# A decoder layer in one kernel: loads on other queues, norms beside the preceding cross-attention, another order of the first rows and another memory layout

## The chip, the cores and the metric

The kernel runs on one core of a Trainium2 chip. The metric is the device time of one execution in microseconds (us). Six actors matter. TensorE (PE) multiplies matrices; its weight loads (PEld) overlap its matmuls. VectorE (DVE) and ScalarE (ACT) do elementwise work and read PE's results out of PSUM. GpSimd (POOL) does some copies and, above all, issues DMAs; SyncE (SP) only issues DMAs. Each of them works through its own instructions in order, so that an instruction which waits holds up all that stand behind it on that engine. The 16 DMA engines of the core move the data.

## The reference: what is computed

`x` is 4 batches of 512 rows of 512 numbers. Three blocks with residuals are added to it:

```python
x = x + attn(layernorm(x), Wq, bq, Wk, bk, Wv, bv, Wo, bo)   # 16 heads of 128
x = x + gamma * xattn(layernorm(x), ctx, ctx)                # 8 heads over 64 rows each
x = x + ffn(layernorm(x), w1, w3, w2)                        # hidden 1365
```

- The self-attention takes, for each head, the softmax over a 128 x 128 matrix: `q` and `k` are contracted over the 512 positions, not over the head's numbers.
- The cross-attention treats each batch as a 512 x 512 matrix, cut into 8 heads of 64 rows. A head's scores are 512 x 512, contracted over its 64 rows.
- In the feed-forward block (FFN) each weight matrix is first made ternary: with s the mean absolute value, `q = clip(round(w / s), -1, 1) * s`. Then `silu(x w1) * (x w3)`, times w2.

## The kernel before, in words

**Number format.** Products that need it are made from three parts of each operand (`h`, `l`, `d`, class `Tri`): one pass of `h` and `l` matmuls into one PSUM bank, one of `d` into another, joined by `total` (L357) on DVE. `products` (L330) does this for a 512 x 512 product in two pairs of row blocks; it is 48 matmuls. At six points in it, it calls `tick()`, through which other work is woven in.

**First phase (`phase_a`).** For each batch `b` the rows are normalized (`normed`, L375) and stored to DRAM (`kept_x`); then a Gram matrix is formed (`gram_upper`, L407, and `gram_rest`, L435). Batch 0 is normalized chunk by chunk under a fixed order on DVE, the other batches at once. Then follow 16 steps (`STEPS`, L858, head group `j` outside, batch `b` inside). A step forms `keys_of` (L470) from the Gram matrix and the key weights, then, one step later, the `scores` (L490) with the query weights and a softmax, and one more step later the transposed result is stored to DRAM (`kept_e`). Weights are loaded by `raw_of` (L232): a 512-row matrix in four chunks of 128 rows by four runs of 512 bytes, and a row `last` that is broadcast. The last chunk's row 127 is then overwritten with the bias by a small DMA from POOL. `fold` (L252) adds a multiple of `last` to each chunk on DVE. Query chunks of the next head group are loaded by SP when the step with `b == 0` has issued its scores, and folded (`queries_folded`, L851) in the step with `b == 1`, after `keys_of`. The value and output weights are cut into their parts beside the steps (`kept_weights`, L276) and stored to DRAM.

**Second phase.** The loop from L966 goes over batches `b` and head groups `j`. Each turn has two products, `values_out` (L455, with the `o` weights) and `values_of` (L480, with the `v` weights); each reads 12 weight tiles of 256 KB, which SP loads into the pool `a_w`. Between them stands `output(*waiting)` (L536), which adds the preceding turn's result to four accumulator tiles `acc`; these start as `x` plus the bias `bo` (`accumulators`, L944, `biased`, L952). After the last head group, `acc` goes to DRAM (`x_a`).

Beside these products run, through `tick()`, two chains of small steps, paced by the class `Side` (L168): `n` steps over `of` ticks.

- `quantize()` (L639) reads the FFN weights twice in pieces through the pool `a_stage` (loads by POOL, `staged`, L571), makes them ternary and stores them.
- `row_norms` (L651) and `cross` (L670) of the *preceding* batch. `row_norms` takes the mean and deviation of each row from `acc`, stores them to DRAM (`norm_a`) and loads them back in another layout (`norms`), all on POOL's queue. `cross` then fetches rows `xd` and `kd` (`fetch`, L685), scales them (`split`, L692: ACT makes `qs` and `kh`, DVE corrects `qs` and makes `kl`), and for each of 8 heads makes scores `xs` (`softmax_rows`, L709), transposes the softmax and weighs the values. The 11 steps of norms and 62 of `cross` together are spread over the 48 ticks of a batch; `side.rest()` at `j == 0` finishes what is left.

**Third phase.** The FFN (L1043) multiplies each batch by `t1` and `t3` (L1058) and `t2` (L1093). The cross-attention of the last batch runs beside batches 0 and 1.

**Order of the work.** The program's order gives each instruction a priority; a scheduler at compile time then orders each engine's instructions by when it thinks their inputs are ready. `tc.issue_after(mark)` keeps what is in its block, as far as it is on the mark's own engine, behind the marked instruction. Pools lie on the left or right end of SBUF like stacks; a pool with `reuse_waits="tile"` that lies on another's former place waits only for the tiles it covers.

Of the kernel before, what the change touches and what calls it, by code (L numbers as in the profile page):

```python
# [11 lines left out]
F32 = mybir.dt.float32  # L12
# [22 lines left out]
H_OF = 1.0 - 0.5**13  # L35
PAD_RIGHT, WIDER = 88, 128


@with_exitstack
def decoder_layer_kernel(  # L40
# [111 lines left out]

    x3p, tp, ep = apool("a_x3", 12), apool("a_t", 3), apool("a_e", 3)
    kept = {
# [77 lines left out]
    def raw_of(n, j, pool, load, bufs):  # L232

        def bring(k):
            t = pool.tile([P, GW], F32, tag=f"raw_{n}", bufs=bufs, name=f"{n}_raw_{j}_{k}")
            load(heads(t), of_heads(w_of[n][:, ts(k, P), :], j))
            if k == KC - 1:
                bias = bqkv[:, ts(KINDS.index(n), GW)].rearrange("(o g) c -> g o c", o=1)
                nc.gpsimd.dma_start(heads(t[P - 1 :, :]), of_heads(bias, j))
            return t  # L240

        last = pool.tile([P, GW], F32, tag=f"last_{n}", bufs=1, name=f"{n}_last_{j}")
        load(heads(last), of_heads(w_of[n][:, D - 1 : D, :], j).to_broadcast([P, NG, DH]))
        return last, bring
# [31 lines left out]
    def kept_weights(pool):  # L276

        def load(dst, src):
            nc.gpsimd.dma_start(dst, src)

        def items():
            for j in range(HG):
                for k in range(KC):
                    yield "o", j, k, None
                for k in CHUNKS:
                    yield "v", j, k, None

        sources = {}

        def bring(n, j, k):  # L290
            if n == "o":
                t = pool.tile([P, GW], F32, tag="raw_v", bufs=3, name=f"o_raw_{j}_{k}")
                load(t, by_group(wo[j * T : (j + 1) * T, :], k))
                return t
            if k == KC - 1:
                sources[j] = raw_of("v", j, pool, load, 3)
            return sources[j][1](k)

        coming = []
        for item in itertools.chain(items(), [None]):  # L300
            if item is not None:
                coming.append((item[:3], bring(*item[:3])))
                if len(coming) < 2:
                    continue
            (n, j, k), t = coming.pop(0)
            gate = gates[0]
            if n == "v":
                fold(k, t, sources[j][0], gate)
            tri = Tri(
                *(pool.tile([P, GW], F32R, tag="made", bufs=5, name=f"{n}{p}_{j}_{k}") for p in "hld")  # L310
            )
            halves_of_weight(tri.h, tri.l, t, gate)
            third_of_weight(tri)
            for p, part in zip("hld", (tri.h, tri.l, tri.d)):
                nc.gpsimd.dma_start(kept[n, j, p][ts(k, P), :], part.bitcast(F32))
            yield
# [40 lines left out]
    def total(dst, h, d):  # L357

        nc.vector.scalar_tensor_tensor(dst, h, 1.0 + 1.0 / S, d, ALU.mult, ALU.add)  # L359

# [14 lines left out]
    def normed(b, xs, by_chunk):  # L375
# [3 lines left out]
        def finish(part, std):  # L379
            rstd = inverse(std, f"a_{b}_{part[0]}")  # L380
            for g in part:
                normalize(xs[g], xs[g], mv[:, g, 0:1], rstd[:, g - part[0] : g - part[0] + 1])
                nc.vector.memset(xs[g][:, D - 1 : D], 1.0)
                nc.gpsimd.dma_start(kept_x[b][ts(g, P), :], xs[g])
# [262 lines left out]
    CROSS_STEPS = 3 * 4 * NC + 14  # L647
    NORM_STEPS = 2 * NG + 3
    norms = {}

# [169 lines left out]
    def rows_given(b):  # L820
        return rows_of(b, xnp, "xn", [by_group(x[b], g) for g in range(NG)])

    xs = rows_given(0)

    mark["std"] = nc.scalar.activation(gam, eps, AF.Sqrt).ins
    idle_ones()
    with tc.manual_schedule(engines={nc.vector.engine}):
        normed(0, xs, True)
    make_identity(nc, ident)
# [5 lines left out]
    keys, queries, ys, es, grams, g3 = {j: {} for j in range(HG)}, {}, {}, {}, {}, {}  # L835
    grams[0] = gram_upper(0, xs)
    raw_k = raw_all("k", 0, krp)
    xs = rows_given(1)
    for k in range(KC):
        keys_halves(0, k, raw_k, gates[0])  # L840
    normed(1, xs, False)
    raw_q = raw_all("q", 0, qp)

    def first_rest():
        g3[0] = gram_rest(0, grams[0])

    grams[1] = gram_upper(1, xs, first_rest)
    keys_thirds(0)
    load(gam, gamma.to_broadcast([P, 1]))

# [13 lines left out]
    def turn(n):  # L864
        j, b = STEPS[n]
        turned(b, j, es.pop(n))

    for n, (j, b) in enumerate(STEPS):
        if n == 4:
            xpool.close()  # L870
            ovp = apool("a_ov", 1, phase_a, side="right")
            side = Side(kept_weights(ovp), KEPT_STEPS, 6 * (len(STEPS) - n) - 4)
        if n < 2:
            xs = rows_given(n + 2)
            normed(n + 2, xs, False)
        ys[n] = keys_of(b, j, g3[b], keys[j], side.tick)
        gates[0] = gate_of(ys[n][3])
        if n < 3:
            g3[n + 1] = gram_rest(n + 1, grams[n + 1])
        if n < 2:  # L880
            grams[n + 2] = gram_upper(n + 2, xs)
        if b == 1:
            queries_folded(j)
        if n > 0:
# [23 lines left out]
    def prepare_ffn(b, rows):  # L908
# [19 lines left out]


    u3p, mp = apool("a_u3", 12), apool("a_m", 4)  # L930
    accp, xnp, bop = apool("a_acc", 8), apool("a_xn_kept", 4), apool("a_bo", 1)
    cpool = [
# [5 lines left out]
        wpools.enter_context(tc.tile_pool(name=n, bufs=k, side="right", reuse_waits="tile"))  # L938
        for n, k in (("a_w", 21), ("a_stage", 3))
    )  # L940
    bo_bc = bop.tile([P, D], F32, name="bo_bc")
    nc.gpsimd.dma_start(bo_bc, bo.to_broadcast([P, D]))

    def accumulators(b):  # L944
        accs = []
        for g in range(NG):
            acc = accp.tile([P, D], F32, tag="acc", name=f"acc_{b}_{g}")
            nc.gpsimd.dma_start(acc, by_group(x[b], g))
            accs.append(acc)
        return accs  # L950

    def biased(accs):  # L952
        with tc.issue_after(mark["copied"]):
            for acc in accs:
                nc.vector.tensor_tensor(acc, acc, bo_bc, ALU.add)

    PRODUCT = 6
    TICKS = 2 * HG * PRODUCT
    quant = Side(quantize(), QUANTIZE_STEPS, B * TICKS - PRODUCT)
    side, waiting, accs = Side(), None, None  # L960

    def tick():
        quant.tick()
        side.tick()

    for b in range(B):  # L966
        for j in range(HG):
            u3 = values_out(b, j, x3, weights("o", b, j, wp), tick)
            if b == 0 and j == 0:
                turn(len(STEPS) - 2)  # L970
                turn(len(STEPS) - 1)
            if waiting:
                output(*waiting)
            if j == 0:
                side.rest()
                if b > 0:
                    side = Side(
                        itertools.chain(row_norms(b - 1, accs), cross(b - 1, *cpool)),
                        NORM_STEPS + CROSS_STEPS,
                        TICKS if b + 1 < B else TICKS - PRODUCT,  # L980
                    )
                accs = accumulators(b)
            if j == HG - 2:
# [3 lines left out]
            elif j == HG - 1:  # L987
# [3 lines left out]
                for _ in range(NC):  # L991
                    next(ffn_0)
            eT = turned_kept(b, j)
            ms = values_of(b, j, weights("v", b, j, wp), u3, tick)
            if j == 0:
                biased(accs)
            waiting = [b, j, eT, ms, accs]
    side.rest()
    quant.rest()
# [15 lines left out]
    def fpool(name, bufs):  # L1015
        return ctx.enter_context(tc.tile_pool(name=name, bufs=bufs, reuse_waits="tile"))

    f1, f3, f2, fwk, fg = (
        fpool("f_w1", 1), fpool("f_w3", 1), fpool("f_w2", 1), fpool("f_work", 2),
        fpool("f_g", 2 * NHC),  # L1020
    )
# [14 lines left out]
    for i in range(NHC):  # L1036
        r = min(P, HID - i * P)
        load(t2[:r, i, :].bitcast(F32), kept_t["w2"][i * P : i * P + r, :])
    side = Side(
        itertools.chain([None] * 9, cross(B - 1, *cpool)), CROSS_STEPS + 9, 2 * (NHC + NC) + 2  # L1040
    )

    for b in range(B):  # L1043
# [3 lines left out]
        for i in range(NHC):  # L1047
            if b + 1 < B and i == 2:
                if b + 2 == B:
                    side.rest()  # L1050
                coming = Side(prepare_ffn(b + 1, rows_f(b + 1)), PREPARE_STEPS, NHC - 3)
            r = min(P, HID - i * P)
            hs = []
            for t, n in ((t1, "h1"), (t3, "h3")):
# [10 lines left out]
                hs.append(ph)  # L1065
            sl = fwk.tile([P, T], F32, tag="sl", name=f"sl_{b}_{i}")
            mark["copied"] = nc.scalar.activation(  # L1067
                sl[:r, :], hs[0][:r, :], AF.Silu, scale=scales["w1"][:r, 2:3]
            ).ins
            gf = fwk.tile([P, T], F32, tag="gf", name=f"gf_{b}_{i}")  # L1070
            nc.vector.scalar_tensor_tensor(  # L1071
# [5 lines left out]
            g.append((gh, gl))  # L1077
            side.tick()
            coming.tick()
# [3 lines left out]
        for c in range(NC):  # L1083
            if b == B - 1:
                y = last_ys[c]
            else:
                y = fwk.tile([P, D], F32, tag="y", bufs=1, name=f"yo_{b}_{c}")
                load(y, x_c[b][ts(c, P), :])
# [12 lines left out]
            nc.sync.dma_start(out[b, ts(c, P), :], y)  # L1101
            side.tick()
            coming.tick()
# [47 lines left out]
```

## Time and profile before

| | us |
|---|---|
| Median of 3 runs (range) | 1228.7 (1222.69 to 1229.71) |
| The profiled execution's own time | 1230.62 |
| Its span | 1228.9 |

Busy time of the engines by stage (us), with PE's granted clock and what the DMAs moved:

| Stretch (us) | what runs | PE | DVE | ACT | clock | DMA GB/s |
|---|---|---|---|---|---|---|
| 0 to 33 | first rows | 25.80 | 26.96 | 11.53 | 0.95 | 298 |
| 33 to 120 | steps of head group 0 and on | 87.00 | 54.17 | 35.62 | 1.00 | 102 |
| 120 to 310 | the other head groups, `v` and `o` weights | 182.49 | 130.30 | 77.22 | 0.98 | 253 |
| 310 to 445 | second phase, batch 0 | 127.91 | 94.71 | 38.14 | 0.95 | 321 |
| 445 to 600 | batch 1, cross-attention of 0 | 137.32 | 121.39 | 85.46 | 0.93 | 251 |
| 600 to 770 | batch 2, cross-attention of 1 | 154.63 | 130.72 | 89.24 | 0.95 | 263 |
| 770 to 922 | batch 3, cross-attention of 2 | 138.40 | 113.05 | 86.44 | 0.98 | 222 |
| 922 to 1229 | FFN, cross-attention of 3 | 297.08 | 151.18 | 145.29 | 0.99 | 80 |

A line of the waits reads: engine, line and tile that waited, who ended the wait, then total, times and longest. A line of the timeline reads: start, duration, engine, line and operation, tile written and read, and in brackets the idle time of the engine before it and what ended it. "q" behind an engine's name marks its queue of issued work.

### The profile page before, as it was taken

The page shows a single profiled execution, that of the slowest core. Times are in us where ns is not written, and L with a number is a line of the kernel's source. Part 1 is how long each engine was busy: PE and PEld are TensorE (multiplying, and loading weights), DVE is VectorE, ACT ScalarE, POOL GpSimd, SP SyncE. Part 2 cuts the span into 40 slices and gives each one's busy share as a digit, 9 for nine tenths or more (in the row PEclk, how much of TensorE's full clock was granted, in tenths as well). Part 3 has the DMA queues.
Part 4 walks back from the last instruction along what each step waited for, and adds up shares of the span by engine and source line. Part 5 has one row for each costly group of instructions (what it writes and reads, how often), then busy time and mean ns, then how long its engine had stood idle before and what let it go on. Part 6 is the DMA issues. An engine that isn't in the chain of part 4 may idle for free. (4 is left out here: it accounts for less than half of the span.)

```text
span 1228.9 us, 16751 instructions
## 1 busy us (share of the span) xinstructions
PE 1150.6 (94%) x5406; PEld 888.6 (72%) x5406; DVE 822.5 (67%) x1766; ACT 568.9 (46%) x1141; POOL 312.4 (25%) x556
## 2 busy tenths in 40 slices
PE   7999999999899877999969999898998999999998
PEld 5788787878677655777737766665766877877886
DVE  8557776883667757878667897588875855625232
ACT  3344444532322225675336665275653769833120
POOL 2103444442211233221333322323202211100000
PEclk9999999999899987999979999989998999999999
DMA  9324878777998985878887878867747231121200
GB/s 292 111 60 153 278 239 263 237 255 261 365 316 296 349 306 160 274 233 267 279 270 234 277 236 285 281 212 233 225 161 243 86 112 44 44 94 43 86 9 35
DMA packets 126865, 252.07 MB, mean 205 GB/s; under 512 B 17140, under 2 KB 37924, under 8 KB 126778
## 3 DMA queue, kind: packets, MB, share of 16 engines
q1 hardware_dynamic: 91146, 140.54, 34.5%
q0 software_dynamic: 35632, 110.46, 27.3%
q8 instruction: 43, 0.70, 0.2%
q14 instruction: 44, 0.36, 0.1%
HBM read 196.40 MB, written 54.54 MB: 204 GB/s over the span
## 5 line engine op out<-in xcount | busy, mean ns | idle before, releaser
L1058 PE MATMUL h<-fxh,t 128*128 128x512 f32 (+1 forms) x352 | 141.4, 402 | 5.2 <-DMA t<-t_w 5.2
L1058 PE MATMUL h<-fxl,t 128*128 128x512 f32 (+1 forms) x352 | 139.0, 395 | 0.0
L727 ACT ACTIVATE p<-xs,xnmax 128x512 f32<-128x512 f32 x128 | 87.1, 687 | 62.2 <-PE xp L126 38.2
L721 DVE TENSOR_REDUCE xnmax<-xs 128x1 f32<-128x512 f32 x128 | 84.0, 685 | 15.4 <-PE xs L717 15.3
L1058 PEld LDWEIGHTS h<-fxh,t 128*128 128x128 f32 (+1 forms) x352 | 66.1, 188 | 21.6 <-issue 6.6
L716 PE MATMUL xs<-kh,qs 128*128 128x512 f32 x128 | 51.7, 405 | 30.8 <-DVE qs L700 30.4
L1058 PEld LDWEIGHTS h<-fxl,t 128*128 128x128 f32 (+1 forms) x352 | 66.0, 188 | 15.0 <-DVE acc L540 0.2
L539 PE MATMUL po<-m,eT 128*128 128x512 f32 x128 | 64.6, 649 | 9.0 <-DVE u L359 9.0
L496 PE MATMUL sc<-y,q_raw 128*128 128x128 f32 x512 | 63.0, 280 | 7.5 <-issue 5.1
L126 PEld LDWEIGHTS xp<-ident,p 128*128 128x128 f32 x512 | 59.1, 140 | 15.0 <-DVE acc L540 2.6
L496 PEld LDWEIGHTS sc<-y,q_raw 128*128 128x128 f32 x512 | 62.2, 196 | 10.7 <-issue 5.9
L1093 PE MATMUL y<-t,gh 128*128 128x512 f32 (+1 forms) x176 | 69.3, 394 | 0.0
L191 ACT ACTIVATE uh<-u 128x512 fp32r<-128x512 f32 x64 | 40.3, 631 | 62.5 <-DVE u L359 62.2
L126 PE MATMUL xp<-ident,p 128*128 128x128 f32 x512 | 67.6, 273 | 1.4 <-DVE acc L540 1.4
L1093 PE MATMUL y<-t,gl 128*128 128x512 f32 (+1 forms) x176 | 68.9, 391 | 0.0
L1071 DVE SCALAR_TENSOR_TENSOR gf<-h,scales_w,sl 128x512 f32<-128x512 f32 (+1 forms) x44 | 32.9, 748 | 52.4 <-PE h L1058 47.8
L129 ACT COPY pt<-xp 128x512 f32<-128x512 f32 x96 | 54.3, 591 | 26.8 <-PE xp L126 26.7
L1067 ACT ACTIVATE sl<-h,scales_w 128x512 f32<-128x512 f32 (+1 forms) x44 | 30.3, 689 | 72.6 <-PE h L1058 72.5
L760 PE MATMUL xo<-pt,vals 128*64 128x512 f32 x256 | 58.5, 599 | 0.0
L539 PEld LDWEIGHTS po<-m,eT 128*128 128x128 f32 x128 | 25.7, 207 | 41.1 <-issue 23.4
L679 POOL DMA_DIRECT2D xd<-x_a x64 | 33.9, 534 | 73.0 <-DVE qs L700 52.9
L717 PE MATMUL xs<-kl,qs 128*128 128x512 f32 x128 | 51.2, 402 | 1.2 <-DVE kl L704 1.1
(256 smaller groups left out, 3002.0 us busy)
## 6 DMA issues: line engine op xcount, KB each, us to landing
oh<-kept_oh SPq DMA_DIRECT2D x64, 256.0 KB, 6.4
ol<-kept_ol SPq DMA_DIRECT2D x64, 256.0 KB, 6.4
od<-kept_od SPq DMA_DIRECT2D x64, 256.0 KB, 5.0
vh<-kept_vh SPq DMA_DIRECT2D x64, 256.0 KB, 6.2
vl<-kept_vl SPq DMA_DIRECT2D x64, 256.0 KB, 6.1
vd<-kept_vd SPq DMA_DIRECT2D x64, 256.0 KB, 5.1
kd<-in_kv_dram POOLq DMA_DIRECT2D x64, 128.0 KB, 3.9
xd<-x_a POOLq DMA_DIRECT2D x64, 128.0 KB, 3.2
```

Of the source, the lines that this page charges most:

```text
L126: nc.tensor.transpose(pt[:, ts(k, P)], src[:, ts(k, P)], ident)
L129: nc.scalar.copy(dst, pv)
L191: nc.scalar.mul(tri.h, src, H_OF)
L496: nc.tensor.matmul(sc[:, ts(g, DH)], lhsT=w[k][:, ts(g, DH)], rhs=ys[k][:, ts(g, DH)], start=(k == 0), stop=(k == KC - 1),)
L539: nc.tensor.matmul(po, lhsT=eT[:, ts(g, DH)], rhs=ms[g], start=True, stop=True)
L716: nc.tensor.matmul(sc, lhsT=q[:, ts(m, P)], rhs=kh, start=True, stop=False)
L717: nc.tensor.matmul(sc, lhsT=q[:, ts(m, P)], rhs=kl, start=False, stop=True)
L721: nc.vector.reduce_max(nmax[:, i : i + 1], scs[i], axis=AX.X)
L727: nc.scalar.activation(p, scs[i], AF.Exp, bias=nmax[:, i : i + 1], scale=xscale, accum_out=den[:, i : i + 1],)
L760: nc.tensor.matmul(po[half, :], lhsT=vals[c][:, l, half], rhs=pt[j][:, l, :], start=(l == 0), stop=(l == NC - 1),)
L1058: nc.tensor.matmul(ph[:r, :], lhsT=t[:, block(i, k)], rhs=fxT[j][:, k, :], start=(k == 0 and j == 0), stop=(k == KC - 1 and j == 1),)
L1093: nc.tensor.matmul(py, lhsT=g[i][j][:r, ts(c, P)], rhs=t2[:r, i, :], start=(i == 0 and j == 0), stop=(i == NHC - 1 and j == 1),)
```

## The change

- `HOLE`: an unused tile of 18 KB a partition and `bo_bc` lie where `t3` of the FFN will lie; the pools `a_t` and `a_e` move to the right side, stay open, and serve the FFN's `sl`, `gf` and `y`, whose own pool goes away. `a_e` has 2 buffers in place of 3, `made` 6 in place of 5, `a_w` 18 in place of 21, `a_stage` 6 in place of 3.
- The last chunk of each `q`, `k` and `v` group is loaded without row 127 (127 rows).
- Batches 1 to 3 are normalized on ACT, with `-mean * rstd` as bias, and not on DVE.
- Rows of batches 1 and 2 are loaded ahead of the key weights, those of batch 3 ahead of the query weights; Gram matrices of batches 1 and 2 come ahead of the keys, that of batch 3 in step 1.
- In the steps with `b == 1` the queries are folded at the fourth tick of `keys_of`.
- `acc` and `bo_bc` are loaded by SP, a batch ahead; `biased` stands behind the last `total` on DVE and not behind an instruction of ACT. `kept_e` is loaded ahead of `values_out`.
- A third chain, `aside`, makes the norms and the first six steps of `cross` in 12 ticks, while `side` still runs the preceding batch's cross-attention; `side` then takes the remaining 56 steps over 48 ticks, from `j == 1` to `j == 0` of the next batch. What is left of batch 2's runs in the first nine ticks of the FFN. `quant` starts after the first `values_out`.

```diff
-    x3p, tp, ep = apool("a_x3", 12), apool("a_t", 3), apool("a_e", 3)
+    tp, ep = (
+        ctx.enter_context(tc.tile_pool(name=n, bufs=k, side="right", reuse_waits="tile"))
+        for n, k in (("a_t", 3), ("a_e", 2))
+    )
+    x3p = apool("a_x3", 12)
...
-            load(heads(t), of_heads(w_of[n][:, ts(k, P), :], j))
+            rows = P if k < KC - 1 else P - 1
+            load(heads(t)[:rows], of_heads(w_of[n][:, k * P : k * P + rows, :], j))
...
+            if not by_chunk:
+                mean = mv[:, :, 0:1].rearrange("p g s -> p (g s)")
+                nc.vector.scalar_tensor_tensor(mean, mean, -1.0, rstd, ALU.mult, ALU.mult)
             for g in part:
-                normalize(xs[g], xs[g], mv[:, g, 0:1], rstd[:, g - part[0] : g - part[0] + 1])
+                if by_chunk:
+                    normalize(xs[g], xs[g], mv[:, g, 0:1], rstd[:, g - part[0] : g - part[0] + 1])
+                else:
+                    nc.scalar.activation(
+                        xs[g], xs[g], AF.Identity, bias=mv[:, g, 0:1], scale=rstd[:, g : g + 1]
+                    )
...
+    xs += [rows_given(1), rows_given(2)]
     raw_k = raw_all("k", 0, krp)
-    xs = rows_given(1)
-    for k in range(KC):
-        keys_halves(0, k, raw_k, gates[0])
-    normed(1, xs, False)
+    xs += [rows_given(3)]
     raw_q = raw_all("q", 0, qp)
+    load(gam, gamma.to_broadcast([P, 1]))
+    normed(1, xs[1], False)
...
-    grams[1] = gram_upper(1, xs, first_rest)
+    grams[1] = gram_upper(1, xs[1], first_rest)
+    normed(2, xs[2], False)
+    for k in CHUNKS:
+        keys_halves(0, k, raw_k, gates[0])
     keys_thirds(0)
-    load(gam, gamma.to_broadcast([P, 1]))
+    grams[2] = gram_upper(2, xs[2])
...
-        ys[n] = keys_of(b, j, g3[b], keys[j], side.tick)
+        if n == 1:
+            normed(3, xs[3], False)
+        ys[n] = keys_of(b, j, g3[b], keys[j], ticks_with(4 if b == 1 else 0))
...
-        if b == 1:
-            queries_folded(j)
...
-        for n, k in (("a_w", 21), ("a_stage", 3))
+        for n, k in (("a_w", 18), ("a_stage", 6))
...
-            nc.gpsimd.dma_start(acc, by_group(x[b], g))
+            load(acc, by_group(x[b], g))
...
-        with tc.issue_after(mark["copied"]):
+        with tc.issue_after(mark["total"]):
...
-            u3 = values_out(b, j, x3, weights("o", b, j, wp), tick)
+            if b == 0 and j == 0:
+                wo_tiles = weights("o", b, j, wp)
+                accs = accumulators(0)
+                load(bo_bc, bo.to_broadcast([P, D]))
+            else:
+                if j == HG - 1 and b + 1 < B:
+                    next_accs = accumulators(b + 1)
+                eT = turned_kept(b, j)
+                wo_tiles = weights("o", b, j, wp)
+            u3 = values_out(b, j, x3, wo_tiles, tick)
...
-            if j == 0:
+            if j == 0 and b > 0:
+                aside.rest()
+                crossing = itertools.chain(row_norms(b - 1, accs), cross(b - 1, *cpool))
+                aside = Side(itertools.islice(crossing, AHEAD), AHEAD, 2 * PRODUCT)
+                accs = next_accs
+            if j == 1 and b > 0:
                 side.rest()
-                if b > 0:
-                    side = Side(
-                        itertools.chain(row_norms(b - 1, accs), cross(b - 1, *cpool)),
-                        NORM_STEPS + CROSS_STEPS,
-                        TICKS if b + 1 < B else TICKS - PRODUCT,
-                    )
-                accs = accumulators(b)
+                side = Side(crossing, NORM_STEPS + CROSS_STEPS - AHEAD, TICKS)
...
+    LEFT = (NORM_STEPS + CROSS_STEPS - AHEAD) * 3 * PRODUCT // TICKS
+    crossing = itertools.chain([None] * 11, cross(B - 1, *cpool))
+    before = Side(itertools.chain(side.steps, [None] * LEFT), LEFT, 9)
+    aside = Side(itertools.islice(crossing, AHEAD), AHEAD, 9)
...
+    last = Side(crossing, CROSS_STEPS - 6, 2 * (NHC + NC) + 2 - 9)
```

## The prediction

> **What bounds the kernel now.** I read the page first, then who TensorE (PE) waits for, then the timeline around its longest wait, then the busy times by stage. Busy shares and clock come first:
>
> ```profile
> span 1228.9 us, 16751 instructions
> PE 1150.6 (94%) x5406; PEld 888.6 (72%) x5406; DVE 822.5 (67%) x1766; ACT 568.9 (46%) x1141; POOL 312.4 (25%) x556
> PEclk9999999999899987999979999989998999999999
> ```
>
> PE is the bound: it idles 78.3 us of 1228.9. The change adds and removes no matmul, so it can only win idle time and the low clock that follows a long idle. Who ended PE's waits (total, times, longest, all in us but the times):
>
> ```profile
> PE xs L716 <- DVE qs L700: 30.4, 3, 17.1
> PE po L539 <- DVE u L359: 9.0, 2, 5.8
> PE pg L414 <- DVE xn L383: 5.5, 2, 5.1
> PE h L1058 <- DMA t<-t_w: 5.2, 1, 5.2
> PE sc L496 <- issue: 5.1, 2, 2.7
> ...
> PE sc L496 <- ACT oh L257: 2.4, 1, 2.4
> ```
>
> Three waits, one at the start of each batch's cross-attention, are 30.4 us of it. The timeline of the longest (start, duration, idle time before in brackets):
>
> ```profile
> 443.85 0.69 DVE L955 TENSOR_TENSOR acc<-acc,bo_bc 128x512 f32<-128x512 f32 x1 [5.67 <-DMA acc<-in_x_dram]
> ...
> 453.65 0.55 POOL L663 DMA_DIRECT2D norm_a<-mv_c  x1
> ...
> 460.07 1.40 POOL L666 DMA_DIRECT2D norms<-norm_a  x2 [4.60 <-DMA norm_a<-mv_c]
> ...
> 469.62 0.79 PE L716 MATMUL xs<-kh,qs 128*128 128x512 f32 x1 [17.14 <-DVE qs L700]
> ```
>
> Row norms go to DRAM and back: 453.65 to 469.62 is 16.0 us. Ahead of it DVE stood 5.67 us behind a bias add whose acc load was late. What the idle costs afterwards (PE busy; later PEclk, DMA share, GB/s), with one early stretch for the DMA price below:
>
> ```profile
> 10.00:20.00 10.00, 6.11 (x23) 3.75 (x21) 9.74 (x24) 4.65 (x10) 1.69 (x4) 1.00 1.03 342
> ...
> 460.00:470.00 10.00, 0.38 (x1) 0.38 (x2) 4.46 (x9) 2.87 (x5) 3.72 (x7) 0.50 0.63 204
> 470.00:480.00 10.00, 10.00 (x26) 5.85 (x26) 9.47 (x19) 5.32 (x9) 3.47 (x7) 0.72 0.28 79
> ```
>
> After the gap PE is busy 10 us at clock 0.72: 2.8 us more lost. Last, the query weights of one head group in the first phase:
>
> ```profile
> 121.65 2.52 SPq L199 DMA_DIRECT2D q_raw<-in_wq_dram  x4
> ...
> 127.10 0.52 POOL L239 DMA_DIRECT2D q_raw<-in_bqkv_dram  x1 [2.76 <-DMA q_raw<-in_wq_dram]
> ...
> 135.20 2.74 DVE L254 SCALAR_TENSOR_TENSOR q_raw<-q_last,gate,q_raw 128x512 f32<-128x512 f32 x4
> ```
>
> They are issued 13.5 us before their folds; sc then waits 2.4 to 2.7 us, three times.
>
> **The change, part by part.** The sum starts at the profiled execution: 1230.6 us with a span of 1228.9, which is 1.9 above the median of the runs, 1228.7.
>
> *1. Norms and start of the cross-attention.* The 17 first steps (11 of norms, 6 of fetch, settle and split) still run in the 12 ticks after the batch's first output; the first xs moves from tick 12 to tick 13, behind output(b,0). That alone is little: 8 matmuls at 0.23 and four fp32 ones in 1.9 (row at 793.67), some 3.7 us. The rest comes from the queues. The bias adds now stand behind total on DVE (before, the mark was an ACT instruction and ordered nothing there), which takes 5.67 and 2.5 us of waiting out of the chain; the 16 acc loads leave POOL (16 x 0.54 us issue); six stage buffers in place of three relieve POOL's waits for them (77.4 + 42.1 us), behind which norm_a, norms and xd queue, and DVE's (7.91 us at 628.86 in batch 2's gap). From batch 2 on, the preceding cross-attention runs on through these ticks and fills PE. In batch 1: norms' inputs ready near 440, plus 16.0, is 456; PE reaches xs at 452.5 + 3.7. The three waits are 30.4, and the low clock after them 2.8 (470 to 480), 3.3 (630 to 640: 7.02 busy at 0.53) and 2.8 (800 to 810: 8.60 at 0.67): 39.3. Ends: nothing to 39.3. I take 34, as batch 1 has no slack left.
>
> A rule here: acc loads took a median of 7.0 us on POOL, xn loads of the same size 4.3 on SP. The Trainium skill (DMA: Bandwidth & Descriptors, "Issuing engines are not separate DMA queues") says that all issuers share the same 16 DMA engines, so that moving a load saves only issue time. By it the 1 MB of accs per batch now stands ahead of 12 weight loads on SP, and part 1 would hold only through its order, not through bandwidth.
>
> *2. Late xd and pieces.* po's 9.0 are ACT waiting for xd (7.3 us at 799.12), DVE behind it; pu_2h's wait of 2.3 is DVE behind a weight piece (3.99 at 664.76). POOL's relief and 56 steps in 48 ticks, not 73, give xd more time. Ends 0 and 11.3; I take 5.
>
> *3. FFN start.* t1's place is x3's, free early: its loads go at 890. t3's overlaps t, e and u3 and is loaded only from 923.35. With the hole it lies over x3's end, bo_bc and an unused tile. 5.2 us, and 9.66 busy at 0.68 from 930 to 940: 3.1. Ends 0 and 8.3; I take 8. The 21 cross steps moved into the FFN take the same PE time there; ACT has 5.5 to 10 us in ten busy there today, in nine ticks of 3.6 us it has room.
>
> *4. First rows.* x of batches 1 and 2 is loaded ahead of the key weights; batch 2's 16 gram matmuls (4.6 us) come ahead of the keys, where PE idles 5.1 today. DVE is full there (9.74 and 9.54 of 10 us, 10 to 30) and gives 8 normalizations of 0.55 to ACT. Against it the key weights land about 2 MB / 300 GB/s = 7 us later. Ends: 8 won, 3 lost; I take 5 won.
>
> *5. 127-row loads.* The last chunk of each q, k and v group is loaded without its bias row: 12 loads, 8 on SP, 4 on POOL. POOL's bias load no longer waits (2.76 above). No row shows a load of 127 rows in 512-byte pieces. Lower end: it lands like today's (k_raw 6.4, q_raw 7.5 us); then folds at tick 4 take away the sc waits, 5.1 + 2.4 = 7.5 us won. Upper end: one DMA engine carries it all. The stretch 10:20 gives 342 / 1.03 / 16 = 20.8 GB/s an engine, so 260 KB takes 12.5 us in place of 0.8: it lands at 6.4 + 11.7 = 18.1, the three chunks behind it on that queue near 20.5, folds end at 23.2, not 16.3. 7 us x 3 groups = 21 on PE; v chunks, folded 14.9, 15.0 and 10.8 us after issue (155.62, 203.10, 244.06), come 3, 3 and 7 us late and the first 10: 23 on DVE, half of it on PE, 12; the first keys, behind the same load, 4; DMA that shares that engine, 10. Together 47 lost. The nearest row by row count, 85 rows in 2 KB pieces, is 4.8 us against 4.6 to 6.0 for 128 rows, nearer to the lower end, but other in its pieces; I take the middle of the two ends, 20 lost.
>
> Rule against the change: the same page ("Why a DMA increments its semaphore by 16 and not by 1") says that the slowest dimension of the transfer picks the largest number of engines up to 16 that divides it, and names 127 partitions as one engine. By it the result ends near 1228 in place of 1201; by today's landing near 1173.
>
> *6. Buffers.* The weight pool shrinks from 21 tiles to 18: three fewer loads ahead per product. Today h and l land in 6.4 us median, and a product of 48 matmuls at 0.23 lasts 11; the seventh load goes when pair 1 has used k = 0, about 7.4 us before need. In batch 0 (DMA share 0.91, 310 to 445) eight products could each be 0 to 2 us late: 0 to 16; I take 4. eT loads move ahead of a product on POOL with two buffers, freed one product earlier: hidden under that product; uncovered, one landing of 4.2. gam and bo_bc on SP: used much later; 5.3 us if not. y with two buffers: DVE's 18.6 us of waits, PE does not wait there: 0.
>
> Sum: 1230.6 - 34 - 5 - 8 - 5 + 20 + 4 = 1202.6; less 1.9 for the median: 1201.
>
> **Rivals.** *Loads as today* (parts 1 to 4 hold, part 5 at its lower end): 1201 - 27.5 = 1173. For it: the 85-row row. Against: those pieces are 2 KB.
> *The norm chain still ends last.* 16.0 us of DRAM trip against about 16 of PE work in batch 1; if each start keeps two thirds of its 39.3 (26), 1201 + 21 = 1222. For it: nothing shortens the two DMAs. Against: mv was ready at 450.26 only because DVE stood behind acc.
> *Slower: late 127-row loads.* Mechanism: fold(q), now at tick 4, stands on DVE ahead of the second pair's y totals and blocks them until the chunk lands. At 47 lost 1201 + 27 = 1228; the POOL stores of this phase (DMA share 0.76, 120 to 310) share that engine, and if they double the 12.5 us the three groups lose 12 each more, less some overlap: 1252. It decides from a landing beyond some 27 us.
>
> **How the numbers follow.** Chances: forecast 45%, loads as today 20%, norm chain 15%, late loads 20%. One per cent is 12 us, about what a measurement of this kernel can tell from no change: bounds 1216 and 1241. Faster: 35 of the 45, 20, 3, 0 = 58%. Same: 10, 0, 9, 4 = 23%. Slower: 0, 0, 3, 16 = 19%. Range: 1160 (parts 1 to 5 at their good ends, 1229 - 39 - 11 - 8 - 8 + 0 = 1163) to 1250, leaving out half of the late loads; the forecast's own range is 1180 to 1228.
>
> **What would show it.** Right: PE's wait for qs under 8 us in total, no clock of 0.5 to 0.7 between 445 and 810, no PE wait for t_w, PE idle well under 78. Part 5: landing of the last q chunk (6 or 18 us), sc's wait for DVE fold. Part 6: SP loads of kept_oh ending PE waits in batch 0. Wrong: qs waits stay, or stage 120 to 310 grows by more than 40.

## The result, and the profile after

The changed kernel takes 1281.18 us (median of 4 runs, 1276.71 to 1283.18); the kernel before took 1229.12 beside it (1222.69 to 1229.71). The ratio is 1.043, with a 95% interval of 1.039 to 1.048: slower by some 52 us, where 28 us faster was forecast. The page of the profiled execution:

```profile
span 1281.4 us, 16699 instructions
PE 1161.5 (91%) x5406; PEld 896.6 (70%) x5406; DVE 819.1 (64%) x1757; ACT 576.7 (45%) x1156; POOL 316.6 (25%) x539
PEclk8999788799799999799998899999998999999999
```

PE idles 120 us of the span in place of 78, and the low clock now lies mostly in the first third. Who ended PE's waits in the changed kernel:

```profile
PE sc L512 <- DVE rden L536: 25.3, 2, 13.3
PE sc L512 <- DVE q_raw L260: 17.9, 4, 14.4
PE pg L430 <- DVE xn L399: 13.9, 2, 13.5
PE pu_1h L343 <- DMA oh<-kept_oh: 7.6, 1, 7.6
PE po L555 <- DVE u L365: 5.9, 2, 5.3
PE h L1110 <- DVE gf L1123: 4.7, 1, 4.7
```

The three waits of `xs` for `qs`, 30.4 us, are gone, and so is the wait for `t_w`. In their place stand waits of the first phase: `sc` and `pg`. (`rden` is a small step that stands on DVE behind the folds of `q`; where PE's wait is put down to it, DVE had stood for `q` just before.) The last `sc` matmul starts at 373.5 us, before at 301.8: the first phase is 71.7 us longer. From there to the end it is 907.9 us, before 927.1: 19.2 shorter. The timeline of the first such place after the start of the `v` weights (POOL, SP, DVE and PE rows; duration in the second column):

```profile
121.30 4.58 POOL L285 DMA_DIRECT2D v_raw<-in_wv_dram  x1
...
129.83 28.72 SPq L204 DMA_DIRECT2D q_raw<-in_wq_dram  x4
...
141.42 0.75 DVE L260 SCALAR_TENSOR_TENSOR v_raw<-v_last,gate,v_raw 128x512 f32<-128x512 f32 x1 [12.92 <-DMA v_raw<-in_wv_dram]
...
160.78 1.41 DVE L260 SCALAR_TENSOR_TENSOR q_raw<-q_last,gate,q_raw 128x512 f32<-128x512 f32 x2 [11.43 <-DMA q_raw<-in_wq_dram]
...
162.29 1.47 PE L512 MATMUL sc<-y,q_raw 128*128 128x128 f32 x4 [12.03 <-DVE rden L536]
```

DVE stands 12.92 us for `v` and 11.43 us for the 127-row chunk of `q`, and PE behind it. The fold that starts after the first wait is that of a 128-row chunk of `v`, issued behind the 127 rows: it landed at 141.40, the 127 rows at 140.47. Around the other two loads of `q` for a next head group `sc` waits 13.3 and 14.4 us, and in the first rows DVE stands 13.71 us for the 127-row chunk of `k`, and PE 13.5 us at `pg` behind it.

The four loads of `q`, issued in 2.52 us before, take SP 28.72 us: the first, of 127 rows, takes 0.25 us, the one behind it 26.91. All loads of `q` by SP, and of `v` by POOL (duration of an issue in ns, least, median and most):

```profile
L204 SPq DMA_DIRECT2D q_raw<-in_wq_dram x16: 248/652/26910, 30.1 to 326.7; - x16
...
L285 POOL DMA_DIRECT2D v_raw<-in_wv_dram x16: 759/759/4582, 121.3 to 336.7; - x16
```

What the DMA engines do from 120 to 142 us (the transfers view; each digit of the first row is the busy share of 0.55 us in tenths; in the last rows KB and us to landing):

```profile
DMA  9997899910002111111111126875000000000000
GB/s 387 328 156 223 343 425 410 410 67 22 0 8 12 12 19 27 34 27 26 26 27 27 19 49 204 302 292 196 17 25 18 24 25 17 25 18 24 19 24 23
...
q1 hardware_dynamic: 54, 0.03, 0.4%
...
v_raw<-in_wv_dram POOLq DMA_DIRECT2D x1, 256.0 KB, 15.0
...
v_raw<-in_wv_dram POOLq DMA_DIRECT2D x1, 254.0 KB, 19.2
q_raw<-in_wq_dram SPq DMA_DIRECT2D x1, 254.0 KB
```

And two stretches of it by busy times (after the engines' busy times: PE's clock, DMA share, GB/s):

```profile
136.00:138.00 2.00, 2.00 (x10) 1.68 (x9) 0.00 (x0) 0.00 (x0) 0.00 (x0) 1.00 0.06 21
...
141.00:144.00 3.00, 0.00 (x0) 0.00 (x0) 2.58 (x5) 0.53 (x1) 0.92 (x2) 1.00 0.07 22
```

A share of 0.06 is one engine of sixteen, and 21 GB/s is what it moves: 254 KB take it some 12 us. POOL's load comes first; SP's queue (q1) moves 0.03 MB in the 22 us; after `v` has landed at 140.47 the same share of 0.07 carries `q`, which lands at 160.64, 30.8 us after its issue. A load of all 128 rows that POOL issued behind (256 KB) takes 15.0 us too.

How many engines share a load can be read more directly for the loads that SP issues. The trace holds the updates of the semaphore that tells of each landing. For 128 rows they are sixteen steps as the data lands; for each of the eight loads of 127 rows there is one update half a microsecond after the issue and then a single one at the end, as of one engine.

### The profile page after: what moved, and what is told of

Its sections match the earlier page's. It is cut to its first block, busy times and chain, and to the rows that moved or that the text cites. A ratio compares the mean times of both kernels' runs of the same rounds, so it can differ in the third digit from the quotient of the medians.

```text
span 1281.4 us, 16699 instructions
## 1 busy us (share of the span) xinstructions
PE 1161.5 (91%) x5406; PEld 896.6 (70%) x5406; DVE 819.1 (64%) x1757; ACT 576.7 (45%) x1156; POOL 316.6 (25%) x539
## 4 chain that ended last, share of the span: by engine, by line
PE 55%; DMA 18%; DVE 10%; issue 9%; ACT 4%; POOL 2%; SPq 1%; DVEq 0%; POOLq 0%; ACTq 0%
PE h L1110 11%; PE y L1145 6%; PE xo L777 4%; DMA xd<-x_a 3%; PE sc L512 3%; PE xp L127 3%; PE pg L430 2%; DMA q_raw<-in_wq_dram 2%; PE po L555 2%; DMA t_w<-tern_w 2%; DMA k_raw<-in_wk_dram 2%; DMA v_raw<-in_wv_dram 2%; DMA kept_od<-od 2%; SPq L204 1%; PE xs L733 1%
## 5 line engine op out<-in xcount | busy, mean ns | idle before, releaser
L512 PE MATMUL sc<-y,q_raw 128*128 128x128 f32 x512 | 70.0, 299 | 43.3 <-DVE rden L536 25.3
L512 PEld LDWEIGHTS sc<-y,q_raw 128*128 128x128 f32 x512 | 67.7, 213 | 47.0 <-issue 41.2
L127 PEld LDWEIGHTS xp<-ident,p 128*128 128x128 f32 x512 | 59.2, 140 | 13.5 <-issue 3.2
L555 PE MATMUL po<-m,eT 128*128 128x512 f32 x128 | 60.3, 611 | 5.9 <-DVE u L365 5.9
L1119 ACT ACTIVATE sl<-h,scales_w 128x512 f32<-128x512 f32 (+1 forms) x44 | 30.4, 690 | 61.0 <-PE h L1110 60.8
L756 ACT ACTIVATE p<-p,xrden 128x512 f32<-128x512 f32 x64 | 47.0, 734 | 9.2 <-DVE xrden L754 8.7
L430 PE MATMUL pg<-xn 128*128 128x512 f32 (+3 forms) x128 | 38.0, 453 | 13.9 <-DVE xn L399 13.9
```

The source lines that it names most:

```text
L127: nc.tensor.transpose(pt[:, ts(k, P)], src[:, ts(k, P)], ident)
L430: nc.tensor.matmul(pg[m][:, : D - m * P], lhsT=xs[g][:, ts(m, P)], rhs=xs[g][:, m * P :], start=(g == 0), stop=(g == NG - 1),)
L512: nc.tensor.matmul(sc[:, ts(g, DH)], lhsT=w[k][:, ts(g, DH)], rhs=ys[k][:, ts(g, DH)], start=(k == 0), stop=(k == KC - 1),)
L555: nc.tensor.matmul(po, lhsT=eT[:, ts(g, DH)], rhs=ms[g], start=True, stop=True)
L756: nc.scalar.mul(ps[1], ps[1], rden[:, 1:2])
```

## The experiments

Ratios are to the kernel before, run beside each on the same chip, with 95% intervals.

**1. All 128 rows again.** One part of the change undone.

```diff
-            rows = P if k < KC - 1 else P - 1
-            load(heads(t)[:rows], of_heads(w_of[n][:, k * P : k * P + rows, :], j))
+            load(heads(t), of_heads(w_of[n][:, ts(k, P), :], j))
```

> The changed kernel with one part undone: the last chunk of each q, k and v group is loaded with all 128 rows again. Theory (the 127-row loads lose the time, each carried by one DMA engine and holding up the loads issued behind it): the first phase, whose last score matmul of the first-phase kind moved from 301.8 to 373.5 us, comes back to about 300, and the kernel to some 1281 - 72 = 1209, between 1190 and 1215. Rival 1 (the other order of the first rows, the fold at tick 4 and the queues lose it): over 1260. Rival 2 (the first phase comes back, but the second phase was only fast because the first was slow): 1220 to 1235.

1205.8 us, ratio 0.979 (0.976 to 0.981). The last `sc` starts at 301.9. Against the changed kernel's ratio of 1.043 that is 0.0645 x 1229 = 79 us for twelve loads. Rival 1 falls; rival 2 too. Of PE's waits at `sc` and `pg`, 57.1 us in the changed kernel, 9.7 are left.

**2. The kernel before, with 127 rows.** The reverse of that diff, in the kernel before.

> The kernel before with this one part of the change: the last chunk of each q, k and v group loaded without row 127. Theory (the 127-row loads alone are enough): 60 to 80 us slower than before, 1290 to 1310; the folds stand behind keys_of here, so a little of the wait may be hidden that the fold at tick 4 shows. Rival (it needs the fold at tick 4, which stands on DVE ahead of the second pair): under 1255.

1318.7 us, ratio 1.071 (1.068 to 1.075): 87 us slower, more than expected. PE's waits in it:

```profile
PE sc L497 <- DVE q_raw L255: 40.0, 4, 13.3
PE xs L717 <- DVE qs L701: 31.5, 3, 17.3
```

The old waits for `qs` are still there, the new ones for the folds stand beside them: the loads need nothing else of the change to do their harm. Whether the fold at tick 4 makes it smaller isn't shown, as by the intervals 87 is 83 to 92 and the 79 of experiment 1 some 73 to 86.

**3. The same 127 rows as 112 and 15.**

```diff
-            rows = P if k < KC - 1 else P - 1
-            load(heads(t)[:rows], ...)
+            for lo, hi in ((0, P),) if k < KC - 1 else ((0, 112), (112, P - 1)):
+                load(heads(t)[lo:hi], of_heads(w_of[n][:, k * P + lo : k * P + hi, :], j))
```

> The changed kernel with the same 127 rows in two loads, of 112 and of 15 rows, 12 loads more in all. Theory (what counts is how many DMA engines share a load, and 112 and 15 rows go to 16 and 15 of them): within 8 us of the kernel with 128 rows. Rival (what counts is that the row count isn't 128, or that the bias row's small load no longer waits for the chunk): stays over 1260.

1198.3 us, ratio 0.973 (0.971 to 0.976). The `v` loads land in 5.0 us (median; least and most beside it):

```profile
DMA to landing us min/median/max: 3.9/5.0/7.4
```

So neither the missing row nor the bias that needn't wait is at fault, only the cut. It is even 0.0053 x 1230 = 6.5 us below the kernel with 128 rows, and the intervals just don't meet. The small bias loads on POOL no longer wait for the chunk, which may be the reason; no run shows that alone.

**4. 127 rows for `v` alone**, whose loads POOL issues; `q` and `k` with 128 rows.

```diff
-            rows = P if k < KC - 1 else P - 1
+            rows = P - 1 if k == KC - 1 and n == "v" else P
```

> The changed kernel with 128 rows for q and k, whose loads SP issues, and 127 rows for v, whose loads POOL issues, 4 loads of 12. Theory (one DMA engine whichever queue issues): 4 waits of DVE of some 10 us for the first v chunk, half of it on PE: 15 to 35 us slower than the kernel with 128 rows throughout. Rival (loads that POOL issues are cut over 16 engines in another way, so that only SP's lose): within 5 us of the kernel with 128 rows.

1237.9 us, ratio 1.005 (1.003 to 1.008): 0.0265 x 1230 = 33 us above experiment 1 for four loads, so the eight of SP cost the other 46, if the two add. The 127-row loads of `v` land 18 to 20 us after issue here too.

**5. `acc` loads behind the `o` weights.** The kernel of experiment 3 has a new wait of PE for `oh` (6.44 us). Its timeline there (SP, POOL, PE and DVE rows):

```profile
409.79 0.32 SPq L204 DMA_DIRECT2D ol<-kept_ol  x1
420.41 5.44 SPq L204 DMA_DIRECT2D acc<-in_x_dram  x3
425.94 0.38 SPq L204 DMA_DIRECT2D oh<-kept_oh  x1
...
420.68 1.07 POOL L558 DMA_DIRECT2D x_a<-acc  x2
...
429.94 0.80 PE L343 MATMUL pu_1h<-oh,xh 128*128 128x512 f32 x1 [6.44 <-DMA oh<-kept_oh]
...
441.39 0.16 DVE L602 TENSOR_TENSOR norms<-norms,one 128x1 f32<-128x1 f32 x1 [8.77 <-DMA norms<-norm_a]
```

The `acc` loads for batch 2, which the scheduler put this early, wait for the buffers of batch 0, which its stores to `x_a` still read (SP's waits for `x_a<-acc` are 23.2 us in all). On POOL that wait held up POOL; on SP it holds up the weight loads, 10.6 us. By stretch, PE is busy 3.56 us of ten, and then 9.31 at a clock of 0.57:

```profile
420.00:430.00 10.00, 3.56 (x17) 2.63 (x15) 4.46 (x8) 0.00 (x0) 4.45 (x8) 0.92 0.79 253
430.00:440.00 10.00, 9.31 (x22) 5.72 (x23) 0.35 (x3) 1.17 (x2) 2.69 (x4) 0.57 1.05 348
```

The edit, on the kernel of experiment 3 (`mark["loaded"]` is the last weight load on SP):

```diff
-                if j == HG - 1 and b + 1 < B:
-                    next_accs = accumulators(b + 1)
                 eT = turned_kept(b, j)
                 wo_tiles = weights("o", b, j, wp)
+                if j == HG - 1 and b + 1 < B:
+                    with tc.issue_after(mark["loaded"]):
+                        next_accs = accumulators(b + 1)
```

> The kernel of 112 and 15 rows (1198.3 us), with the next batch's acc loads put behind the o weights of the same turn on SP; in it, as in the changed kernel, they stand ahead of weights, and SP waits 10.6 us (409.79 to 420.41) for the stores of batch 0's acc before it may load into their buffers. Theory (that wait is what makes the o weights late): PE's wait for oh, 6.4 us, goes, and with it the stretch at clock 0.57 behind it (4.3 us): 1187 to 1190. Rival (the weight pool, 18 tiles in place of 21, is too small): the wait for oh stays above 4 us, and the time within 4 us of 1198.

1194.9 us, ratio 0.971 (0.967 to 0.974); its interval overlaps that of experiment 3. The wait for `oh` is gone, as expected, but most of the gain isn't there. Its timeline (POOL, DVE and PE rows):

```profile
436.10 0.54 POOL L680 DMA_DIRECT2D norm_a<-mv_c  x1
...
442.90 1.40 POOL L683 DMA_DIRECT2D norms<-norm_a  x2
...
445.98 0.16 DVE L602 TENSOR_TENSOR norms<-norms,one 128x1 f32<-128x1 f32 x1 [20.29 <-DMA norms<-norm_a]
...
448.20 1.22 PE L555 MATMUL po<-m,eT 128*128 128x512 f32 x1 [12.26 <-DVE u L365]
```

DVE now stands 20.29 us for `norms`, ahead of the total `u`, and PE 12.26 us for `u`. Behind the wait that was taken away stood the norm chain.

**6. 21 weight tiles and 3 stage buffers**, on the kernel of experiment 3.

```diff
-        for n, k in (("a_w", 18), ("a_stage", 6))
+        for n, k in (("a_w", 21), ("a_stage", 3))
```

> The kernel of 112 and 15 rows with the pools as before, 21 weight tiles and 3 stage buffers. Rival (the pool of 18 makes the o weights late): PE's wait for oh falls under 2 us, 1187 to 1192. Theory (SP's wait at the acc loads does): the wait for oh stays near 6, and the time lies between 1196 and 1206, as POOL waits for 3 stage buffers again.

1197.4 us, ratio 0.973 (0.969 to 0.977). The time is as my theory had it, the wait for `oh` is not: it went. SP stands even longer at `acc` (from 408.26 to 421.81), but three tiles more were loaded ahead of it, so `oh` was there. So the late `oh` needs the wait on SP and, it seems, the smaller pool; the number of stage buffers was changed in the same run, and nothing tells the two apart. And again the norm chain takes its place:

```profile
444.59 0.16 DVE L602 TENSOR_TENSOR norms<-norms,one 128x1 f32<-128x1 f32 x1 [13.20 <-DMA norms<-norm_a]
...
446.70 3.78 PE L555 MATMUL po<-m,eT 128*128 128x512 f32 x4 [5.66 <-DVE u L365]
```

**7. `xb_f` ahead of `t2`.** At the FFN's start the kernel of experiment 3 shows (SP, DVE and PE rows):

```profile
866.84 5.53 SPq L204 DMA_DIRECT2D t<-t_w  x11
874.08 0.38 SPq L204 DMA_DIRECT2D xb_f<-x_c  x1
...
887.80 1.29 DVE L96 BATCH_NORM_STATS2 st_f<-xb_f 128x6 f32<-128x512 f32 x2 [7.65 <-DMA xb_f<-x_c]
...
890.45 0.80 PE L1110 MATMUL h<-fxh,t 128*128 128x512 f32 x1 [5.76 <-DVE gf L1123]
```

`t3` is loaded early now, so `t2`'s loads go ahead of the 1 MB of `xb_f`, which lands 13.7 us after its issue; before, `xb_f` went at 910.81, ahead of the loads that still waited for `t3`'s place.

```diff
+    ahead = rows_f(1)
     for i in range(NHC):
         r = min(P, HID - i * P)
         load(t2[:r, i, :].bitcast(F32), kept_t["w2"][i * P : i * P + r, :])
...
-                coming = Side(prepare_ffn(b + 1, rows_f(b + 1)), PREPARE_STEPS, NHC - 3)
+                coming = Side(prepare_ffn(b + 1, rows_f(b + 1) if b else ahead), PREPARE_STEPS, NHC - 3)
```

> The kernel of 112 and 15 rows, with the FFN rows of batch 1 (xb_f) loaded ahead of t2, not behind its 11 loads. Theory (now that t3 is loaded early, xb_f queues behind t2 and lands 13.7 us after its issue, and DVE waits 7.65 us for it ahead of gf): PE's waits for gf and sl at the FFN's start, 5.8 and 2.1 us, and the clock of 0.70 behind them go: 1187 to 1192. Rival (the cross-attention steps moved into the FFN's first nine ticks fill DVE and ACT): the waits stay, within 3 us of 1198.

1196.4 us, ratio 0.972 (0.969 to 0.976). PE's wait for `gf` is gone from the list, and the FFN of batch 0 takes 95.2 us from first `h` to the next batch's first, not 100.9. PE still waits 2.1 us for `sl` and 2.5 us for `p`. As a whole it can't be told from experiment 3: the place is explained, its price is under what was expected.

**8. Without the third chain.** On the kernel of experiment 3, norms and cross-attention follow each other over the batch's 48 ticks as before the change, and the FFN takes none of batch 2's.

```diff
-            if j == 0 and b > 0:
-                aside.rest()
-                crossing = itertools.chain(row_norms(b - 1, accs), cross(b - 1, *cpool))
-                aside = Side(itertools.islice(crossing, AHEAD), AHEAD, 2 * PRODUCT)
-                accs = next_accs
-            if j == 1 and b > 0:
-                side.rest()
-                side = Side(crossing, NORM_STEPS + CROSS_STEPS - AHEAD, TICKS)
+            if j == 0 and b > 0:
+                side.rest()
+                side = Side(itertools.chain(row_norms(b - 1, accs), cross(b - 1, *cpool)),
+                            NORM_STEPS + CROSS_STEPS, TICKS if b + 1 < B else TICKS - PRODUCT)
+                accs = next_accs
```

> The kernel of 112 and 15 rows without the third chain: norms and cross-attention of the preceding batch follow each other over the 48 ticks of a batch as before the change, and the FFN takes none of batch 2's. All else stays. Theory (the preceding cross-attention that runs on fills PE at the starts of batches 2 and 3): waits of 10 to 15 us at their first xs come back, with a lower clock behind them: 1206 to 1218. Rival (the earlier accs, the bias behind total and the freed POOL queue gained it all): within 4 us of 1198.

1204.3 us, ratio 0.979 (0.975 to 0.983), against 0.973 (0.971 to 0.976): some 6 us, and the intervals overlap. In the profiled execution, which was the fastest of the five (1196.7 us), PE's waits for `qs` come back with

```profile
PE xs L733 <- DVE qs L717: 5.7, 3, 2.5
```

and not with 10 to 15 us, let alone the 30.4 of before. So most of what the three waits lost was won by the other parts of the change, the queues and the order on DVE among them, and not by the chain that runs on. Both theories were wrong in part.

**9. `norm_a` and `norms` of batch 0 issued by ACT**, on the kernel of experiment 5.

```diff
-        nc.gpsimd.dma_start(norm_a[b].rearrange("(p g) s -> p g s", g=NG), mv)
+        issuer = nc.gpsimd if b else nc.scalar
+        issuer.dma_start(norm_a[b].rearrange("(p g) s -> p g s", g=NG), mv)
...
-            nc.gpsimd.dma_start(norms[b][half], ...)
+            issuer.dma_start(norms[b][half], ...)
```

> The kernel with the acc loads behind the o weights (1194.9 us), with norm_a and norms of batch 0 issued by ACT and not by POOL; there POOL issued norm_a at 436.10, behind xd's wait for the stores of x_a and two t_w, and norms at 442.90, DVE stood 20.29 us for norms, and PE 12.3 us for the total u behind it. Theory (that POOL queue ends the norm chain last, as the rival 'norm chain still ends last' has it, at the first of the three starts): PE's wait for u falls under 4 us and the clock of 0.50 behind it goes: 1178 to 1186. Rival (the two DMAs take so long under load that the order on POOL matters little): the wait moves, and the time stays between 1190 and 1198.

1193.2 us, ratio 0.970 (0.966 to 0.973), not told from experiment 5. Its timeline (ACT, DVE and PE rows):

```profile
419.02 0.39 ACTq L681 DMA_DIRECT2D norm_a<-mv_c  x1
425.42 1.56 ACTq L684 DMA_DIRECT2D norms<-norm_a  x2
...
435.06 0.16 DVE L602 TENSOR_TENSOR norms<-norms,one 128x1 f32<-128x1 f32 x1 [7.02 <-DMA norms<-norm_a]
...
437.06 1.12 PE L555 MATMUL po<-m,eT 128*128 128x512 f32 x2 [2.38 <-DVE u L365]
```

The chain starts 17 us earlier and ends 11 us earlier; PE's wait of 12.26 us becomes 2.38, as expected. But the time lies in the rival's range. The trip itself, from the issue of `norm_a` to `norms` on DVE, now takes 16.0 us (419.02 to 435.06), with the DMA engines full (share 1.06). In experiment 5 it took 9.9 (436.10 to 445.98, share 0.88), and in the kernel before 13.0 (453.65 to 466.69, share 0.94). And of what was won PE loses 5.0 us again at `pm_1h`, which waits for `uh` of ACT. POOL's queue was the wait here; little hung on it.

**10. Experiments 5, 7 and 9 together.**

> The same kernel with the FFN rows of batch 1 loaded ahead of t2 as well. Theory (the gains of separate places add): 2 to 6 us below the kernel with norm_a and norms on ACT. Rival (each place's gain is given back at the next wait): within 2 us of it.

1191.3 us, ratio 0.967 (0.964 to 0.971): the fastest kernel of the study, 39 us under the kernel before. The last step is 2 us, less than can be told.

**11. Other cuts of the 127 rows:** `q` 125 and 2, `k` 126 and 1, `v` 113 and 14; the program ran once.

```diff
-            rows = P if k < KC - 1 else P - 1
+            cut = {"q": 125, "k": 126, "v": 113}[n]
+            for lo, hi in ((0, P),) if k < KC - 1 else ((0, cut), (cut, P - 1)):
```

> The changed kernel with the 127 rows cut in other ways: q 125 and 2, k 126 and 1, v 113 and 14. Theory (the number of DMA engines is the largest divisor of the row count up to 16: 14 for 126, 5 for 125, 1 for 113): k's first loads land like those of 128 rows, q's 125 rows within 3 to 6 us of the others', v's 113 rows some 12 to 20 us after their issue as in the changed kernel; time near that of 127 rows for v alone, 1230 to 1245. Rival (every row count that is no multiple of 16 goes to one engine): all three are late, over 1265.

1233.0 us, as expected. PE's waits of `sc` for the folds of `q` are 5.9 us in all, as with 128 rows (6.0): 125 rows do no harm that shows. The 113 rows of `v` do: DVE stands 11.2, 7.9 and 11.5 us for `v` in three of the four groups, and PE's longest wait, 11.6 us at `sc`, which the profile puts down to no one, begins during the last of these. The first of the four (the transfers view from 112 to 124 us):

```profile
v_raw<-in_wv_dram POOLq DMA_DIRECT2D x1, 226.0 KB, 17.3
v_raw<-in_wv_dram POOLq DMA_DIRECT2D x1, 28.0 KB, 13.4
```

So it isn't that a count must be a multiple of 16, and the rival falls. The Trainium skill's page DMA: Bandwidth & Descriptors (section "Why a DMA increments its semaphore by 16 and not by 1") has the largest divisor up to 16 set the number of engines; by it that is 14 for 126, 5 for 125 and 1 for 113 and 127. The trace agrees: the semaphores of SP's loads tell of 126 rows in 14 late steps, of 125 rows in 5, and of 127 rows, in the changed kernel, in one. Loads by POOL end in sixteen steps whatever their rows, so that for 113 rows, and for 127 of `v`, only the late landing and the share of 0.06 speak.

## Why the prediction was wrong

**The step that failed is part 5, "127-row loads".** It had both ends and the rule, and took "the middle of the two ends, 20 lost", for which the only row was one of 85 rows "but other in its pieces". Measured: 79 us against loads of 128 rows (experiment 1), 87 in the kernel before (experiment 2). So the loss lies not between the two ends but beyond the upper one, 47.

The row of 85 rows couldn't decide. 85 is 5 times 17, so that by the rule that the prediction quotes five engines share such a load; it says nothing of one engine. And a test of the rule lay in the trace of the kernel before: the semaphore of SP's 85-row load (`t` at 940.11) tells of its landing in five late steps, those of 128 rows in sixteen.

The rate of the upper end was right: 20.8 GB/s for an engine was estimated, 21 and 22 are shown, so that 254 KB take some 12 us. Three things on top of it were not:

- The landing was put at 18.1 us, with 10 us in all for other transfers on that engine. SP's eight loads of 127 rows landed 14.2 to 30.8 us after their issue: 14.2 in a quiet stretch (82.78), 30.8 at 129.83, where `v` went first. At 225.09 no 127-row load of `v` is outstanding, yet `q` took 23.7 us: in the first 12 of them POOL's queue moved 3.44 MB and SP's 0.07. The deciding point that the rival named, "a landing beyond some 27 us", was passed at one load of `q`; its cause, other transfers on the same engine, fits that at 225.09 too, but no run takes these transfers away.
- SP's issuing itself was blocked: behind each of its eight loads of 127 rows, SP's next issue took 10.4 to 26.9 us. The prediction had the loads behind land near 20.5 us; behind the `q` of 129.83 the first landed after 31.1, and the other two were issued only 27 us later. No term was there for that.
- POOL's issue of a 127-row load takes 4.58 us and not 0.76, in each of the four. No term was there for that either.

The slower rival, "late 127-row loads", was thus the mechanism, with its place (the fold ahead of the second pair) and sign. It had 20% and a price of at most 1252 us, and the sign of being wrong that the prediction named, over 40 us more from 120 to 310, came too: the first phase grew by 71.7. 79 in place of 20 is 59 of the 80 us between 1201 and 1281; the rest of the sum, below, is about the other 21. The lower end, 7.5 won from the waits of `sc`, isn't reached in any run: these waits are 6.0 us in experiment 1 and 4.0 in experiment 3.

**The rest of the sum.** Without part 5 it says 1201 - 20 = 1181, with the lower end 1173; experiments 1 and 3 give 1205.8 and 1198.3. By stretches between first matmuls of a kind (us), the kernel before against that of experiment 3, whose profiled execution was its slowest (1203.2 us); steps of the cross-attention that moved to a later stretch are in the differences too:

| Stretch | before | 112 + 15 rows | |
|---|---|---|---|
| to the last `sc` | 301.8 | 291.4 | -10.4 |
| to the first `po` of batch 0 | 40.7 | 39.0 | -1.7 |
| to that of batch 1 | 129.0 | 113.0 | -16.0 |
| to that of batch 2 | 163.7 | 161.0 | -2.7 |
| to that of batch 3 | 158.5 | 160.7 | +2.2 |
| to the first `h` of the FFN | 129.1 | 106.3 | -22.8 |
| to the end | 306.1 | 330.1 | +24.0 |

*Part 1* (34 predicted): the mechanism is right, the size isn't. The waits for `qs` went, in the changed kernel and in experiment 3. The start of batch 1 won 16.0. The stretches to batches 2 and 3 together win next to nothing: around their starts PE waits for `keys` (2.9), `xc` (2.0, 2.1) and `u` (4.8, 3.9) instead. Moving `acc` to SP was counted as 16 issues off POOL; that its buffers wait for stores, and what on SP would queue behind that, was not asked. Experiments 5, 6 and 9 show that three waits lie one behind another here: `acc` on SP, POOL's queue, and the DRAM trip. The rival "norm chain still ends last" holds in that sense. The trip's 16.0 us, a term of both, were misread: 453.65 to 469.62 ends with PE's first `xs`, while `norms` was on DVE at 466.69. The trip took 13.0 us there, and 9.9 to 16.0 in experiments 5 and 9.

*Part 2* (5): not settled. The waits of `po` for `u` are 9.0 us before, 8.8 in experiment 3 and 1.6 in experiment 1.

*Part 3* (8): wrong as a sum. `t_w` went with its 5.2 and 3.1 us, but the loads that go earlier push `xb_f` behind `t2` (experiment 7); with 5.8, 2.1 and 1.8 us of new waits nothing is won. The cross-attention moved into the FFN only moves: -22.8 and +24.0.

*Part 4* (5): the first `sc` starts at 69.8 in place of 73.3 in experiment 3, at 73.4 in experiment 1: 3.5 or nothing.

*Part 6* (4, ends 0 and 16): in the changed kernel 7.6 us at one product, with a clock of 0.52 from 510 to 520 us, not small losses at eight. The pools are part of its cause at most, the wait on SP the other (experiments 5 and 6).

## What to carry to other kernels

Before the row count of a DMA is changed, ask how many engines can share the new count: 127 rows in place of 128 cost 79 us in twelve loads, and 112 + 15 rows cost nothing. Where a rule and a row of the profile seem to disagree, ask first whether the row tests the rule. A load that one engine carries is not only late itself: what is issued behind it on its queue is late too, and sometimes what the other queue issues. When a load moves to another queue, look at what its buffer waits for, since that wait moves along and stands ahead of other things there; and when a wait is removed, price the next one behind it before the whole of it is counted as won.

## What was not expected of the hardware

- SP's issuing stands still behind such a load: the next issue took 10.4 to 26.9 us behind all eight in the changed kernel and 12.7 to 25.9 behind the eight of experiment 2; no other issue of SP took more than 6.2 us in these two kernels.
- On POOL it is the issue of the load itself that grows: 4.58 us for 127 rows and 4.14 for 113 (experiment 11), 0.76 for 128, and 0.73 for 112 (experiment 3).
- From 130 to 140 us the loads of POOL and SP didn't run beside each other: with both outstanding, 0.06 of the DMA engines moved 21 GB/s, and SP's queue 0.01 MB. It isn't always so: from 310 to 317 us, with `v` and `q` outstanding again, POOL's queue moved 0.16 MB and SP's 0.10. The Trainium skill's page DMA: Bandwidth & Descriptors (section "Issuing engines are not separate DMA queues") says that the issuers share the same engines; that both loads used the same one at the first place is shown only by that share.
- The same page (section "Why a DMA increments its semaphore by 16 and not by 1") tells of an exception, in which some loads that GpSimd issues spread 127 partitions over all 16 engines. These loads, of four runs of 512 bytes a partition, didn't: 19.2 us for 254 KB, at a share of 0.06.
